# Sixteen-bit column addresses and 44 copied columns a step in a graph-network layer

## The chip, the cores and the metric

One core of one Trainium2 chip. The metric is the device time of one execution in microseconds (us). Three executions of the kernel before took 1896.46, 1897.21 and 1897.28 us; the median is 1897.21.

The engines: PE (TensorE) multiplies matrices, DVE (VectorE) and ACT (ScalarE) copy and do arithmetic by elements, POOL (GpSimd) issues the gathers, SP (SyncE) issues the other transfers. Each has its own queue of instructions and runs it in order. An engine's queue also runs instructions that touch no data path, such as loads of registers (TENSOR_LOAD); the profile shows these under DVEq, ACTq and so on, and doesn't count them as busy.

## What is computed

One layer of message passing on a graph of 12500 nodes with 64 features and 212500 edges with 32 features, sorted by destination, then a residual and a normalization:

```python
def _mlp(x, W1, b1, W2, b2):
    return jax.nn.relu(x @ W1 + b1) @ W2 + b2
msg_in = jnp.concatenate([nodes[row], nodes[col], edge_features], axis=-1)
messages = _mlp(msg_in, mW1, mb1, mW2, mb2)
aggregated = jax.ops.segment_sum(messages, col, num_segments=nodes.shape[0])
upd_in = jnp.concatenate([nodes, aggregated], axis=-1)
return _mlp(upd_in, uW1, ub1, uW2, ub2)
...
x = _layernorm(x + _L0_gnn_ref(...), axis=-1)
```

Here `row` is `src` and `col` is `dst`. All numbers are float32. The costly part is `nodes[row]`: for each edge the 64 features of its source, at an address that only the data tells.

## The kernel before

The edges are cut into 554 groups of 384 (G, GE), each of three tiles of 128 edges. The main loop (L560) makes one step for each group. Step k puts three pieces of work on PE, of three groups: `turn` of group k, `hidden` of group k-2, `sums` of group k-4.

- `gather` (L146): for each tile of a group, POOL issues one indirect DMA (L149) that fetches the 128 source rows from HBM into `own.s`, a ring of eight buffers. A gather of group g waits until PE has turned a group seven or eight before it. Groups are fetched four steps ahead (AHEAD), but POOL's own queue holds nothing besides, so it may run as far ahead as the ring allows.
- `onehot` (L329, VectorE) writes beside the rows, for each edge, which of 32 destinations of the group's window it has.
- `turn` (L341) transposes rows and one-hot columns on PE; ACT copies the result into `own.st` (L351), where a column is an edge: 64 source features, 32 one-hot rows, 32 edge features (these loaded by SP, L289).
- `hidden` (L366) multiplies these columns with the weights on PE; ACT applies the relu (L377).
- `sums` (L394, L399) adds up the messages of each window; VectorE adds them to `agg` and the counts to `own.xc` (L406, L407).
- `places` (L301, L308) and `windows` (L315, L320), once in four steps, prepare the destinations' part of the weights. The starts of four windows are loaded into registers by one TENSOR_LOAD (L301).
- `update` (L413 to L458), some 25 times, finishes 512 nodes: two matmuls, relu, second layer, statistics, normalization, store. Its steps stand in line with the main loop's.

For some groups the first of the three tiles isn't gathered. The list COPIED (L81) names them. The kernel holds all nodes' features transposed in SBUF (`own.xc`, one column of 4 bytes by 64 partitions a node), and `fetch` (L475) copies the sources of such a tile column by column straight into `own.st`: a copy of 64 x 4 bytes from a dynamic address, by VectorE (L503) or by ACT (L505). From step 18 (BEGIN) on each step copies 40 columns (COLS), in four batches: VectorE 8 and 12, ACT 12 and 8. Ahead of each batch one TENSOR_LOAD (issued at L490) reads the batch's addresses from `indices` into as many registers. So of every 3.2 steps one tile is copied and not gathered: 164 tiles, and 1497 gathers are left of 1661. For a copied group ACT's L351 is in two parts, since the copied columns must stay.

The addresses: `indexes` (L462) has SP load the node numbers of eight steps (SPAN) as 32-bit integers, `addresses` (L469, L473 on VectorE) turns them in place into byte addresses (times 4, plus `own.at`), two steps before they are used.

In a step's program order VectorE has L406, L407, in every fourth step L320 four times, then L329, the load and copies of its first batch, the load and copies of its second. ACT has L351, L377, then its two batches. Every engine may run ahead of or behind the others by about two steps, as far as buffers in PSUM and SBUF allow.

Of the kernel before, what the change touches and what calls it, by code (L numbers as in the profile page):

```python
# [11 lines left out]
BF16 = mybir.dt.bfloat16  # L12
I32 = mybir.dt.int32
U8 = mybir.dt.uint8
AF = mybir.ActivationFunctionType
ALU = mybir.AluOpType
ET = mybir.EngineType
# [3 lines left out]
P = 128  # L21
N = 12500
# [9 lines left out]
GE = TG * P  # L32
# [8 lines left out]
NP = N + 44  # L41
# [5 lines left out]
TIMES = 4  # L47
BEGIN = 18
CHECKED = 8
VCOLS = (8, 12)  # L50
ACOLS = (12, 8)
COLS = sum(VCOLS + ACOLS)
SPAN = 8


# [25 lines left out]
COPIED = []  # L81
while BEGIN - (-P * (len(COPIED) + 1) // COLS) < G - SHORT:
    COPIED.append(BEGIN - (-P * (len(COPIED) + 1) // COLS))


class Own:
# [4 lines left out]
    def __init__(self, nc, ctx):  # L91
        def on(name, *shape, of=nc.sbuf_tensor):
            return ctx.enter_context(of(name, list(shape), F32)).ap()

        self.s = [on(f"own_s{i}", P, TG, D + W) for i in range(RING)]
        self.st = [on(f"own_st{i}", P, SB * GE) for i in range(BLOCKS)]
        self.wm = [on(f"own_wm{i}", P, H) for i in range(NW)]
        self.h = [on(f"own_h{i}", P, TG, H) for i in range(NH)]
        self.ident = on("own_ident", P, P)
        self.one = on("own_one", P, 1)  # L100
        self.at = (nc.sbuf_base + 31) // 32 * 32
        self.xc = on("own_xc", P, NP)

        self.ps = [[on(f"own_ps{i}{k}", P, 512, of=nc.psum_tensor) for k in range(3)]
                   for i in range(2)]

# [2 lines left out]
def ordered(ctx: ExitStack, tc: tile.TileContext, a, own, ok):  # L109
# [3 lines left out]
    nc = tc.nc  # L113
# [3 lines left out]
    iop = ctx.enter_context(tc.tile_pool(name="iota_ps", bufs=1, space=PSUM))  # L117
    ups = ctx.enter_context(tc.tile_pool(name="upd_ps", bufs=1, space=PSUM))
    ixp = ctx.enter_context(tc.tile_pool(name="index", bufs=2))
    early = ctx.enter_context(ExitStack())  # L120
    temp = early.enter_context(tc.tile_pool(name="temp", bufs=1))
    ident, wm = own.ident, own.wm
    xc = own.xc[: D + 2]
    xc_bytes = own.xc.bitcast(U8)

# [9 lines left out]
    def after(first, *others):  # L135

        tc.declare_no_dep(first.ins, group="quiet", reason="waits for the last of a step")
        for i in others:
            tc.add_manual_dep(
                first.ins, i.ins.name,  # L140
                mybir.DependencyInfo(mybir.DependencyClass.Sync, mybir.DependencyReason.DATA),
                reason="the kernel's own rings",
            )
        return first
# [77 lines left out]
    for f, (g0, g1) in zip(firsts_f, halves):  # L222
# [20 lines left out]
    nc.scalar.activation(agg.rearrange("p (a b) -> p a b", a=P),  # L243
                         zero.unsqueeze(1).to_broadcast([P, P, NP // P]), AF.Copy)
    wc = const.tile([H, H], F32, name="wc")

    starts, xws, indices, columns_by = {}, {}, {}, {}

    up = None

# [41 lines left out]
    def columns(g):  # L292
        t, c = own.st[g // SB % BLOCKS], (g % SB) * GE
        return t, c, sum(tiles_of(g))
# [40 lines left out]
    def turn(g, ps):  # L335
# [9 lines left out]
        def copy(step):  # L345
# [4 lines left out]
            copies = [  # L350
                after(nc.scalar.activation(t[r, c : c + n][:, m], xt[r, m], AF.Copy), step)  # L351
                for r, m in (apart if g in columned else whole)
# [8 lines left out]
    def hidden(g, ps):  # L361
# [11 lines left out]
        def relu(step):  # L373
            hidden_by[g] = step
            h = own.h[g % NH]
            if len(set(sizes)) == 1:
                relu_by[g] = [nc.scalar.activation(h, pre, AF.Relu)]  # L377
            else:
                relu_by[g] = [nc.scalar.activation(h[:p, j, :], pre[:p, j, :], AF.Relu)
                              for j, p in enumerate(sizes)]  # L380
# [32 lines left out]
    def update(base, p, n):  # L413
# [8 lines left out]
        def first(xin):  # L422
# [3 lines left out]
            u = up.tile([H, CH], F32, name="u")  # L426
            nc.scalar.activation(u[:, :q], u_ps[:, :q], AF.Relu, bias=ub1)  # L427
            nc.vector.tensor_tensor(xin[:p, :n], xin[:p, :n],
# [3 lines left out]
        def second(xu):  # L432
# [12 lines left out]
            rstd = up.tile([P, 4], F32, name="rstd")  # L445
            nc.scalar.activation(rstd[:p, :n], mv[:p, :n, 1], AF.Sqrt, bias=eps[:p])  # L446
            return y, mv, rstd
# [13 lines left out]

    def indexes(i):  # L462

        n = min(SPAN * COLS, P * len(COPIED) - i * SPAN * COLS)
        if n > 0:
            indices[i] = ixp.tile([1, SPAN * COLS], I32, name="index")
            nc.sync.dma_start(indices[i][:, :n], a["src_copied"][:, i * SPAN * COLS :][:, :n])

    def addresses(i):  # L469

        if i in indices:
            t = indices[i][:, : min(SPAN * COLS, P * len(COPIED) - i * SPAN * COLS)]
            nc.vector.tensor_scalar(t, t, 4.0, float(own.at), ALU.mult, ALU.add)  # L473

    def fetch(k):  # L475

        i, n = divmod(k - BEGIN, SPAN)
        if i < 0:
            return
        if n == 0:  # L480
            indexes(i + 1)
        if n == SPAN - 2:
            addresses(i + 1)
        c0 = (k - BEGIN) * COLS
        for engine, count in [*((ET.DVE, c) for c in VCOLS), *((ET.Activation, c) for c in ACOLS)]:
            count = min(count, P * len(COPIED) - c0)
            if count <= 0:
                return
            b = c0 - i * SPAN * COLS
            _, v = nc.values_load_multi_w_load_instructions(  # L490
                indices[i][0:1, b : b + count], engines=[engine],
                min_val=own.at, max_val=own.at + 4 * (N - 1),
                skip_runtime_bounds_check_because="a source is one of the nodes",
            )
            for q, at in zip(range(c0, c0 + count), v):
                g, c = COPIED[q // P], q % P
                t, first_c, _ = columns(g)
                o = t.bitcast(U8)[:D, 4 * (first_c + c) : 4 * (first_c + c + 1)]
                x_at = xc_bytes[:D, bass.ds(at - own.at, 4)]
                by = columns_by.setdefault(g, {})  # L500
                new = engine not in by
                if engine == ET.DVE:
                    by[engine] = nc.vector.tensor_copy(o, x_at)  # L503
                else:
                    by[engine] = nc.scalar.activation(o, x_at, AF.Copy)  # L505
                after(by[engine], *([hidden_by[g - BLOCKS * SB]] if new else []))
            c0 += count

    waiting = [(closes, update(base, p, n)) for base, p, n, closes in PLAN]
    now = []  # L510
# [44 lines left out]
    places(0)  # L555
    windows(0, ups.tile([H, CH], F32, name="u_ps")[:, :H], False)[1]()
    indexes(0)
    made = summed = 0

    for k in range(G):  # L560
        if k < BITS:
            bit(k)
        if k == CHECKED:
            addresses(0)
            combined()
            ordered_edges()
            early.close()
            up = ctx.enter_context(tc.tile_pool(name="upd", bufs=2))
# [8 lines left out]
        else:  # L577
# [6 lines left out]
            for _ in range(2):  # L584
                if made <= k:
                    step((hidden, made))
                    made += 1
        onehot(k + 2)
        fetch(k)
        if k + AHEAD < G:  # L590
            gather(k + AHEAD)
# [285 lines left out]
@with_exitstack  # L877
def gnn_layer(ctx: ExitStack, nc, a):
    own = Own(nc, ctx)
    tc = ctx.enter_context(tile.TileContext(nc))  # L880
    flag = ctx.enter_context(tc.tile_pool(name="flag", bufs=1))
    ok = flag.tile([1, 1], I32, name="ok")
    with tc.manual_schedule():
        ordered(tc, a, own, ok)
    good = nc.values_load(ok[0:1, 0:1], min_val=0, max_val=1,
                          skip_runtime_bounds_check_because="a comparison's result")
    with tc.If(good == 0):
        with tc.manual_schedule():
            unordered(tc, a, own)
# [35 lines left out]
```

## Time and profile before

| | |
|---|---|
| median of three executions | 1897.21 us |
| profiled execution: its time | 1895.48 us |
| its span, first to last instruction | 1893.5 us |
| granted TensorE clock, mean | 0.969 |
| PE, busy | 1361.4 us (72%) |
| VectorE, busy | 1492.9 us (79%) |
| ACT, busy | 1550.7 us (82%) |
| POOL, busy | 1417.6 us (75%) |
| gathers (L149) | 1497, 946 ns each |
| column copies by VectorE (L503) | 10500, 897.7 us busy |
| column copies by ACT (L505) | 10492, 1057.1 us busy |
| ACT's copy of a turned group (L351): 96x384; 96x256 and 32x128 | 480 ns; 379 and 268 ns |
| address computation (L473) | 66, 0.37 us each |

How to read the views. A group's line has: code line, engine, operation, tile written <- tiles read, count | busy us, mean ns of one instruction | idle time of the engine just before, and what ended most of it. "issue" means that the engine waited for nothing that the profile shows: its queue was busy with something else, for example with a load of registers. A timeline line has start, duration, engine, line, operation, count, and in brackets the idle time before. Copies overlap on an engine: one lasts 190 ns from start to end, but the next starts some 80 ns after it (twelve take about 1.0 us), so busy time divided by count is below the mean. A line of a table by stretches has for each engine busy us and count, then clock, DMA share and GB/s. A line of a source's instructions has count, then shortest, median and longest in ns, then first and last start.

### The profile page before, as it was taken

The numbers are of one execution on the slowest core, as the hardware profiler recorded it, in microseconds if no ns is written. First come the engines' busy times: TensorE is split into PE (matmuls) and PEld (weight loads), VectorE is DVE, ScalarE is ACT, GpSimd is POOL, SyncE is SP. The second block draws the span as 40 slices with busy tenths as digits, with TensorE's granted clock in tenths as the row PEclk, the third lists the DMA queues.
The fourth block names the chain that finished last, engine by engine and source line by source line (L and its number), as shares of the span: only waits on it lengthen the run. The fifth ranks groups of instructions, "written<-read, shape, count | busy, mean of one in ns | idle before, by whom it ended". The sixth has DMA issues, their size and how long they took to land. (4 is left out here: it accounts for less than half of the span.)

```text
span 1893.5 us, 58044 instructions
## 1 busy us (share of the span) xinstructions
PE 1361.4 (72%) x12209; PEld 1193.4 (63%) x12209; DVE 1492.9 (79%) x13761; ACT 1550.7 (82%) x11818; POOL 1417.6 (75%) x1504
## 2 busy tenths in 40 slices
PE   3776777677777777677676776877767767767777
PEld 3666666666666666666665666666666656666665
DVE  3578888778888788887888878878888887888873
ACT  3489889888888888988988888889888888898882
POOL 7777777777777777777777777777777777777774
PEclk9999999999999999999999999999999999999999
DMA  6322222222222222222222222222222222222221
GB/s 136 73 46 45 46 48 44 50 43 48 46 45 48 47 43 50 45 46 44 48 50 43 48 46 45 46 48 44 50 44 47 47 48 44 47 44 50 44 47 29
DMA packets 68440, 92.50 MB, mean 49 GB/s; under 512 B 30893, under 2 KB 38350, under 8 KB 68078
## 3 DMA queue, kind: packets, MB, share of 16 engines
q0 software_dynamic: 47904, 49.12, 14.7%
q1 hardware_dynamic: 19260, 39.12, 7.4%
q14 instruction: 260, 2.13, 0.4%
q8 instruction: 102, 1.67, 0.4%
q10 hardware_dynamic: 914, 0.46, 0.1%
HBM read 85.29 MB, written 3.20 MB: 47 GB/s over the span
## 5 line engine op out<-in xcount | busy, mean ns | idle before, releaser
L149 POOL DMA_INDIRECT own_s<-in_x,src_sb x1497 | 1416.8, 946 | 457.3 <-issue 407.5
L503 DVE COPY own_st<-own_xc 64x4 uint8 x10500 | 897.7, 190 | 231.0 <-issue 217.9
L505 ACT ACTIVATE own_st<-own_xc 64x4 uint8 x10492 | 1057.1, 194 | 18.2 <-issue 15.2
L341 PE MATMUL own_ps<-own_ident,own_s 128*96 128x128 f32 x1661 | 289.5, 285 | 496.0 <-DMA own_s<-in_x,src_sb 157.9
L341 PEld LDWEIGHTS own_ps<-own_ident,own_s 128*96 128x96 f32 x1661 | 169.3, 132 | 566.1 <-ACT own_h L377 240.7
L394 PE MATMUL own_ps<-own_s,own_h 128*128 128x128 f32 x3322 | 480.5, 283 | 4.1 <-ACT own_h L377 2.9
L366 PE MATMUL own_ps<-own_wm,own_st 128*128 128x128 f32 x3322 | 479.4, 283 | 0.0
L351 ACT ACTIVATE own_st<-own_ps 96x384 f32<-96x384 f32 (+2 forms) x718 | 293.2, 408 | 205.8 <-PE own_ps L399 104.7
L394 PEld LDWEIGHTS own_ps<-own_s,own_h 128*128 128x128 f32 x3322 | 432.6, 199 | 6.3 <-ACT own_h L377 4.7
L366 PEld LDWEIGHTS own_ps<-own_wm,own_st 128*128 128x128 f32 x3322 | 432.1, 199 | 1.4 <-issue 0.5
L377 ACT ACTIVATE own_h<-own_ps 128x384 f32<-128x384 f32 x553 | 263.9, 477 | 16.0 <-PE own_ps L366 16.0
L399 PE MATMUL own_ps<-own_s,own_one 128*1 128x32 f32 x3322 | 190.1, 194 | 0.0
L320 DVE COPY own_wm<-own_ps 32x128 f32<-32x128 f32 x550 | 156.9, 285 | 5.6
L399 PEld LDWEIGHTS own_ps<-own_s,own_one 128*1 128x1 f32 x3322 | 114.5, 84 | 69.4 <-issue 6.2
L329 DVE TENSOR_TENSOR own_s<-iota,dlc 128x96 f32<-128x96 f32 x554 | 142.4, 258 | 14.3 <-issue 0.2
L406 DVE TENSOR_TENSOR agg<-own_ps,agg 128x32 f32 x554 | 105.1, 190 | 59.5 <-PE own_ps L399 25.9
L407 DVE TENSOR_TENSOR own_xc<-own_ps,own_xc 1x32 f32 x554 | 101.2, 183 | 30.6 <-PE u_ps L425 11.4
L308 DVE COPY xw<-own_xc 66x32 f32 x554 | 73.0, 207 | 15.5 <-DMA own_xc<-in_xT 9.8
L315 PE MATMUL own_ps<-w1b,xw 66*128 66x128 f32 (+1 forms) x276 | 69.1, 333 | 0.0
L446 ACT ACTIVATE rstd<-mv,eps 128x4 f32<-128x4 f32 (+1 forms) x25 | 7.4, 297 | 55.3 <-DVE mv L444 55.3
L437 PE MATMUL u_ps<-u,u 128*128 128x64 f32 (+1 forms) x196 | 50.1, 399 | 0.5 <-ACT u L427 0.5
L437 PEld LDWEIGHTS u_ps<-u,u 128*128 128x128 f32 (+1 forms) x196 | 47.1, 324 | 2.2 <-ACT u L427 0.9
(62 smaller groups left out, 276.7 us busy)
## 6 DMA issues: line engine op xcount, KB each, us to landing
own_st<-in_efT SPq DMA_DIRECT2D x138, 192.0 KB
own_s<-in_x,src_sb POOLq DMA_INDIRECT x1497
xin<-in_x SPq DMA_DIRECT2D x24, 128.0 KB
out<-o SPq DMA_DIRECT2D x24, 128.0 KB
own_xc<-in_xT SPq DMA_DIRECT2D x12, 179.2 KB
index<-in_src_copied SPq DMA_DIRECT2D x65, 1.2 KB
dlc_i<-in_dst_cols SPq DMA_DIRECT2D x1, 831.0 KB
own_xc<-in_xT SPq DMA_DIRECT2D x4, 179.5 KB
```

The source lines that it names most:

```text
L149: nc.gpsimd.indirect_dma_start(out=s[:p, j, :D], out_offset=None, in_=x[:, :], in_offset=bass.IndirectOffsetOnAxis(ap=src_sb[:p, g * TG + ...
L320: c = nc.vector.tensor_copy(wm[g % NW][D : D + W, :], wp[i * W : (i + 1) * W, :])
L329: places_by[g] = nc.vector.tensor_tensor(own.s[g % RING][:, :, D:], iota.unsqueeze(1).to_broadcast([P, TG, W]), dlc[:, g * TG : (g + 1) * ...
L341: nc.tensor.transpose(xt[:, j * P : j * P + p], s[:p, j, :], ident[:p, :p])
L351: after(nc.scalar.activation(t[r, c : c + n][:, m], xt[r, m], AF.Copy), step)
L366: nc.tensor.matmul(pre[:p, j, :], t[:, c + j * P : c + j * P + p], wm[g % NW], start=True, stop=True)
L377: relu_by[g] = [nc.scalar.activation(h, pre, AF.Relu)]
L394: did.append(nc.tensor.matmul(sg, h[:p, j, :], s[:p, j, D:].unsqueeze(1).to_broadcast([p, TIMES, W]), start=j == 0, stop=j == len(sizes) - 1))
L399: did.append(nc.tensor.matmul(counted, own.one[:p], s[:p, j, D:], start=j == 0, stop=j == len(sizes) - 1))
L406: after(nc.vector.tensor_tensor(agg[:, at], sg[:, 0, :], agg[:, at], ALU.add), step),
L503: by[engine] = nc.vector.tensor_copy(o, x_at)
L505: by[engine] = nc.scalar.activation(o, x_at, AF.Copy)
```

## The change

The addresses become 16-bit integers. `addresses` writes them into a tile of its own (`address`, two buffers), converting on the way; so that the largest address is below 65536, `own.xc` becomes the first tensor in SBUF, and the space at the start of SBUF that is kept for descriptors of POOL's transfers is set to 8 KB a partition, less than by default. A step copies 44 columns: VectorE 16 and 8, ACT 16 and 4, each batch with one load. In the array of node numbers each batch is filled up to a multiple of eight, so that each batch starts at a multiple of 16 bytes (48 slots a step for 44 columns).

```diff
+U16 = mybir.dt.uint16
...
-VCOLS = (8, 12)
-ACOLS = (12, 8)
+VCOLS = (16, 8)
+ACOLS = (16, 4)
 COLS = sum(VCOLS + ACOLS)
+LOADS = 8
+SLOTS = sum(-c // LOADS * -LOADS for c in VCOLS + ACOLS)
...
+        self.at = (nc.sbuf_base + 31) // 32 * 32
+        self.xc = on("own_xc", P, NP)
+        assert self.at + 4 * N <= 1 << 16
         self.s = [on(f"own_s{i}", P, TG, D + W) for i in range(RING)]
...
-        self.at = (nc.sbuf_base + 31) // 32 * 32
-        self.xc = on("own_xc", P, NP)
...
+    adp = ctx.enter_context(tc.tile_pool(name="address", bufs=2))
...
-        n = min(SPAN * COLS, P * len(COPIED) - i * SPAN * COLS)
-        if n > 0:
-            indices[i] = ixp.tile([1, SPAN * COLS], I32, name="index")
-            nc.sync.dma_start(indices[i][:, :n], a["src_copied"][:, i * SPAN * COLS :][:, :n])
+        if i * SPAN * COLS < P * len(COPIED):
+            indices[i] = ixp.tile([1, SPAN * SLOTS], I32, name="index")
+            nc.sync.dma_start(indices[i], a["src_copied"][:, i * SPAN * SLOTS :][:, : SPAN * SLOTS])
...
-            t = indices[i][:, : min(SPAN * COLS, P * len(COPIED) - i * SPAN * COLS)]
-            nc.vector.tensor_scalar(t, t, 4.0, float(own.at), ALU.mult, ALU.add)
+            addresses_by[i] = adp.tile([1, SPAN * SLOTS], U16, name="address")
+            nc.vector.tensor_scalar(addresses_by[i], indices.pop(i), 4.0, float(own.at),
+                                    ALU.mult, ALU.add)
...
-        c0 = (k - BEGIN) * COLS
-        for engine, count in [*((ET.DVE, c) for c in VCOLS), *((ET.Activation, c) for c in ACOLS)]:
-            count = min(count, P * len(COPIED) - c0)
+        c0, b = (k - BEGIN) * COLS, n * SLOTS
+        for engine, most in [*((ET.DVE, c) for c in VCOLS), *((ET.Activation, c) for c in ACOLS)]:
+            count = min(most, P * len(COPIED) - c0)
             if count <= 0:
                 return
-            b = c0 - i * SPAN * COLS
             _, v = nc.values_load_multi_w_load_instructions(
-                indices[i][0:1, b : b + count], engines=[engine],
+                addresses_by[i][0:1, b : b + count], engines=[engine],
...
             c0 += count
+            b += -most // LOADS * -LOADS
...
+    def slots(s):
+        n = -len(s) // (SPAN * COLS) * -SPAN
+        s = padded(s, n * COLS, 0).reshape(n, COLS)
+        parts, c = [], 0
+        for m in VCOLS + ACOLS:
+            parts.append(np.pad(s[:, c : c + m], ((0, 0), (0, -m % LOADS))))
+            c += m
+        return np.concatenate(parts, 1).reshape(1, n * SLOTS)
...
-    nc = bacc.Bacc("TRN2", target_bir_lowering=False, num_devices=1)
+    nc = bacc.Bacc("TRN2", target_bir_lowering=False, num_devices=1,
+                   dynamic_dma_scratch_size=1 << 13)
```

More of the change, by code (lines that the diff above doesn't have):

```diff
@@ L245, in ordered @@
     wc = const.tile([H, H], F32, name="wc")
-    starts, xws, indices, columns_by = {}, {}, {}, {}
+    starts, xws, indices, addresses_by, columns_by = {}, {}, {}, {}, {}
     up = None
@@ L905 @@
         "src": padded(v["src"], NT * P, 0).reshape(NT, P).T,
-        "src_copied": np.concatenate([v["src"][g * GE :][:P] for g in COPIED])[None],
+        "src_copied": slots(np.concatenate([v["src"][g * GE :][:P] for g in COPIED])),
         "dst_cols": padded(v["dst"], G * TG * P, -1).reshape(G * TG, P).T,
```

## The prediction

> **What bounds the kernel now.** I read the page's sums first, then the costliest groups, POOL's waits and timeline, VectorE's waits, and last the loads of registers, which the sums leave out.
>
> ```profile
> PE 1361.4 (72%) x12209; PEld 1193.4 (63%) x12209; DVE 1492.9 (79%) x13761; ACT 1550.7 (82%) x11818; POOL 1417.6 (75%) x1504
> ...
> L149 POOL DMA_INDIRECT own_s<-in_x,src_sb x1497 | 1416.8, 946 | 457.3 <-issue 407.5
> L503 DVE COPY own_st<-own_xc 64x4 uint8 x10500 | 897.7, 190 | 231.0 <-issue 217.9
> ```
>
> ACT looks busiest, but the share of busy time misleads. POOL's 1416.8 busy and 457.3 idle us make 1874 of the span's 1893.5, and the idle part is "issue": it waits for nobody. Its timeline, first in the opening (before any column is copied by VectorE), then in the middle:
>
> ```profile
> 21.30 0.95 POOL L149 DMA_INDIRECT own_s<-in_x,src_sb  x1 [0.30 <-issue]
> 22.55 0.94 POOL L149 DMA_INDIRECT own_s<-in_x,src_sb  x1 [0.30 <-issue]
> ...
> 1002.36 0.94 POOL L149 DMA_INDIRECT own_s<-in_x,src_sb  x1 [0.30 <-issue]
> 1003.60 0.94 POOL L149 DMA_INDIRECT own_s<-in_x,src_sb  x1 [0.30 <-issue]
> 1004.85 0.94 POOL L149 DMA_INDIRECT own_s<-in_x,src_sb  x1 [0.30 <-issue]
> ```
>
> A gather starts every 1.249 us, from the first to the last (1497 x 1.249 = 1870). In POOL's list of waits the longest wait for PE is 0.3 us, the gap that is there anyway, so the ring of eight buffers never holds a gather back. POOL sets the pace; the rest follows, and after the last gather's end (1875.7) some 18 us are left. The chain of waits starts from the last instruction and shows only this tail's engines; it doesn't name POOL.
>
> Second is VectorE, between 80 us (its first column) and 1846 (its last):
>
> ```profile
> 80.00:1846.00 1766.00, 1284.21 (x11584) 1127.82 (x11581) 1442.75 (x13528) 1513.39 (x11756) 1335.36 (x1414) 0.97 0.22 46
> ...
> DVE own_st L503 <- issue: 217.9, 585, 0.9
> ...
> 997.95 0.66 DVE L503 COPY own_st<-own_xc 64x4 uint8 x8 [0.23 <-issue]
> 999.12 1.00 DVE L503 COPY own_st<-own_xc 64x4 uint8 x12 [0.50 <-issue]
> ```
>
> It is busy 1442.75 of 1766, and 231 more go to gaps ahead of the copies, where its queue is reading registers: 95% used, against ACT's 86% (1513) with 15 us of such gaps. So the change must be followed on VectorE, though POOL sets the end.
>
> **Gathers.** The list COPIED grows from 164 tiles (525 steps x 40 / 128) to 180 (525 x 44 / 128), each one gather less: 1497 to 1481. 16 x 1.249 = 20.0 us less on POOL. No queue order changes there.
>
> **Copies.** 180 x 128 = 23040 columns at 44 a step are 523 steps and 28 columns more: VectorE 12576 (+2076), ACT 10464 (-28). On VectorE the 12-run above takes 1.00 us with a 0.15 tail, so a further copy in a run is about 78 ns: 2076 x 0.078 = +162 us. The address computation L473 goes from 320 to 384 elements, 0.37 to about 0.45 us, 66 times: +6. ACT gains 16 split copies of L351 (268 + 379 against 480 ns): +3, less 28 columns. The index load on SP has the same count with 1.5 KB for 1.2, issued eight steps ahead. One wait changes: L473 used to write in place, and now writes a buffer of its own that the loads of the span before the last must have left. Behind it in VectorE's queue stand the step's copies, and PE waits for those; but those loads ended six steps earlier, and ACT runs no more than two or three steps behind VectorE, so I cost it at nothing.
>
> **Loads of registers.** The durations, by line and engine, in narrow windows where the batch is known (4 starts; 8 columns; 12 columns), and a single register at the end:
>
> ```profile
> L301 DVEq TENSOR_LOAD <-start_i x139: 340/344/594, 13.8 to 1863.6; - x139
> ...
> L490 DVEq TENSOR_LOAD <-index x1: 597/597/597, 1002.9 to 1002.9; - x1
> ...
> L490 DVEq TENSOR_LOAD <-index x1: 847/847/847, 1004.2 to 1004.2; - x1
> ...
> L885 DVEq TENSOR_LOAD <-ok x1: 313/313/313, 1887.0 to 1887.0; - x1
> ```
>
> 1, 4, 8, 12 registers: 313, 344, 597, 847 ns. Three registers more cost 31 ns within the first four; each further four cost 250. So the price goes by reads of four 32-bit numbers, 16 bytes, and hardly by registers. The trace cannot say whether a read is 16 bytes or four registers, since all its numbers are 32 bits wide. Bound below: by bytes, 16 sixteen-bit numbers are 597 and 8 are 344 (at 10 ns a register more, some 680 and 385). Bound above: by fours of registers, 847 + 250 = 1097 and 597. I take the lower: one register costs nearly as much as four, as one read of a whole row would, and a rule by registers has to explain why the first four are nearly free.
>
> [...]
>
> What is seen of a load is what its cover leaves. The second load starts some 4 copies before the first batch ends: cover about 0.44 us, and 0.09 from its end to the first copy; 847 + 90 - 440 = 0.50, the gap at 999.12. After: 385 + 90 - 440 = 0.04, so most of the 180 us of these gaps go (the other 46 stand before the first batch). The first load is covered by L406, L407 and L329, 0.85 us when VectorE is behind: 680 + 90 fits. If that cover is gone (VectorE waiting for PE), 0.2 to 0.3 are seen, but then VectorE isn't late. ACT: 12 and 8 at 783 and 545 become 16 and 4, about 630 and 310, under L351 and L377 as now.
>
> **VectorE's new sum.** Busy 1443 + 162 + 6 = 1611, gaps about 35: 1646. From 676.4 to 716.5, where the kernel catches up after an update, VectorE was busy 33.9 and in gaps 5.1 of 40.1 us, 97%: that is how full it can be. 1646 / 0.97 = 1697, against the 1746 that POOL now leaves (1766 - 20). It fits with 49 us to spare; gaps could reach 83 us (0.16 a step) before it binds. ACT with 1516 and PE with 1284 fit.
>
> **Layout.** Own.xc goes first in SBUF so that addresses fit 16 bits, and POOL's scratch for descriptors is cut to 8 KB. I cost both at nothing: two or three gathers are in flight at 1.25 us each. If gathers had to wait for an earlier landing (some 1.6 us after POOL's end, by the first transposes of a group), the pace would go towards 2.5 us.
>
> **Sum.** 1893.5 - 20.0 = 1873.5 span; 1895.48 was that execution's time, 2.0 more, and the median shown is 1.7 above it: 1877.2, or -1.05%. What can be told from no change is 0.2%, 4 us.
>
> **Rivals.**
> 1. Slower: loads priced by fours of registers. Second load 597 + 90 - 440 = 0.25 x 524 = 130 us of gaps. First load 1097 + 90 - 850 = 0.33, on three steps in four (the fourth has L320's 1.18 us as cover): 130. VectorE: 1611 + 260 = 1871, over the 1746, and it decides from 83 us of gaps. Span 80 + 1871 to 1929 (at 97%) + 47.5, about 2000 to 2056; 2025 as time. For: four by four is as good a reading of 313, 344, 597, 847. Against: the nearly free first four.
> 2. The lower price holds, but VectorE's margin of 49 us is eaten: copies at 85 ns (897.7 / 10500) add 15, gaps of 80 instead of 35 add 45, and updates, whose steps run in line on VectorE, do the rest. It paces at (1626 + 80) / 0.97 = 1759, 13 over POOL: 1886 span, 1890; up to 1905. For: 95% used today. Against: today's 97% was reached while PE fed it.
> 3. VectorE's copies hold POOL. If each added copy stopped gathers for its 78 ns: +162 - 20, about 2039. Against: gathers take 0.95 us at 21.30 without columns and 0.94 at 1002 between them. [...]
> 4. The smaller scratch stalls gathers, or something not listed: over 1950.
>
> **How the numbers follow.** Forecast 0.70; rival 2 0.12 (of it 0.06 faster, 0.03 same, 0.03 slower); rival 1 0.13; rival 3 0.02; rival 4 0.03. Faster 0.76, same 0.03, slower 0.21. The range 1868 to 1908 holds the forecast (1872 to 1882 alone) and rival 2, 0.82; the rest lies far above and is left out.
>
> **What would show it.** Right: 1481 gathers, still 1.25 us apart; VectorE's loads near 600 to 700 and 345 to 400; gaps at L503 under 80 us; VectorE busy near 1660 of the span (88%). Wrong: loads near 1100 and 600 with gaps over 250 (rival 1); gathers that wait for PE for microseconds (VectorE or PE paces); gathers longer than 0.95 us (rivals 3, 4).

## The result, and the profile after

The changed kernel takes 3937.86 us (median of 4, 3934.33 to 3943.24) against 1896.84 for the kernel before: 2.076 times as long, 95% interval 2.073 to 2.080. The forecast was 1877. From the page of the changed kernel, the span, the busy sums, and the groups of the gathers and of VectorE's column copies:

```profile
span 3932.6 us, 60013 instructions
...
PE 2142.4 (54%) x12209; PEld 1873.6 (48%) x12209; DVE 1663.5 (42%) x15837; ACT 1597.2 (41%) x11806; POOL 1399.0 (36%) x1488
...
L153 POOL DMA_INDIRECT own_s<-in_x,src_sb x1481 | 1398.2, 944 | 2491.8 <-PE own_ps L403 2078.4
L506 DVE COPY own_st<-own_xc 64x4 uint8 x12576 | 1033.2, 172 | 2124.7 <-issue 1928.3
```

No engine is even 55% busy. The gathers are 16 fewer, as planned, and each lasts what it lasted; but POOL now waits 2078 us for PE. And ahead of VectorE's copies stand 2125 us of gaps in place of 231, again put down to "issue". VectorE's timeline of the changed kernel, two steps with four batches and what lies between:

```profile
2005.59 1.23 DVE L506 COPY own_st<-own_xc 64x4 uint8 x16 [2.70 <-issue]
2007.98 0.69 DVE L506 COPY own_st<-own_xc 64x4 uint8 x8 [1.16 <-issue]
2008.59 0.17 DVE L410 TENSOR_TENSOR agg<-own_ps,agg 128x32 f32 x1
2008.79 0.18 DVE L411 TENSOR_TENSOR own_xc<-own_ps,own_xc 1x32 f32 x1
2008.90 1.18 DVE L324 COPY own_wm<-own_ps 32x128 f32<-32x128 f32 x4
2010.09 0.26 DVE L333 TENSOR_TENSOR own_s<-iota,dlc 128x96 f32<-128x96 f32 x1
2012.48 1.23 DVE L506 COPY own_st<-own_xc 64x4 uint8 x16 [2.13 <-issue]
2015.36 0.66 DVE L506 COPY own_st<-own_xc 64x4 uint8 x8 [1.65 <-issue]
```

What runs in these gaps are the loads of registers (count, then shortest, median, longest in ns), in windows that hold one of each: VectorE's load of 16, its load of 8, and ACT's of 4:

```profile
L493 DVEq TENSOR_LOAD <-address x1: 3589/3589/3589, 2008.8 to 2008.8; - x1
...
L493 DVEq TENSOR_LOAD <-address x1: 1833/1833/1833, 2013.1 to 2013.1; - x1
...
L493 ACTq TENSOR_LOAD <-address x1: 880/880/880, 2008.5 to 2008.5; - x1
```

Sixteen registers take 3589 ns and eight 1833: (3589 - 1833) / 8 = 220 ns a register. Before, 32-bit loads of 8 and 12 took 597 and 847. The profile puts 192 us of the 2125 down to ACT, but counted in the trace, 1041 of VectorE's 1048 loads end less than 0.1 us before the first copy of their batch starts: the copies wait for the loads. Do the gaps account for the time? The table by stretches, from VectorE's first column to its last:

```profile
79.00:3876.00 3797.00, 2058.25 (x11568) 1801.40 (x11563) 1612.19 (x15595) 1559.24 (x11743) 1330.32 (x1411) 0.63 0.10 22
```

VectorE is busy 1612 us there, and with 2125 of gaps its queue is full for 3737 of 3797 us, 98%. Before, it was 1443 + 231 in 1766. So the gaps grew by 1894 and the busy time by 169, together 2063, against 2039 that the span grew. PE stands behind VectorE: its turn of a group (L345) starts 0.10 us after VectorE has written the group's one-hot columns (L333), in 481 of the 514 steps that are left without the first and last 20.

```profile
2017.07 0.26 DVE L333 TENSOR_TENSOR own_s<-iota,dlc 128x96 f32<-128x96 f32 x1
...
2017.43 0.85 PE L345 MATMUL own_ps<-own_ident,own_s 128*96 128x128 f32 x3 [3.16 <-issue]
```

And POOL stands behind PE: bursts of five gathers at the old spacing (the first three and the next burst's first are shown), then a long wait for PE to free a pair of buffers.

```profile
2007.09 0.94 POOL L153 DMA_INDIRECT own_s<-in_x,src_sb  x1 [11.51 <-PE own_ps L403]
2008.33 0.94 POOL L153 DMA_INDIRECT own_s<-in_x,src_sb  x1 [0.31 <-issue]
2009.58 0.94 POOL L153 DMA_INDIRECT own_s<-in_x,src_sb  x1 [0.30 <-issue]
...
2021.52 0.94 POOL L153 DMA_INDIRECT own_s<-in_x,src_sb  x1 [8.49 <-PE own_ps L403]
```

### The profile page after: what moved, and what is told of

It reads as the page before. It is cut to its first block, busy times and chain, and to the rows that moved or that the text cites. A ratio compares the mean times of both kernels' runs of the same rounds, so it can differ in the third digit from the quotient of the medians.

```text
span 3932.6 us, 60013 instructions
## 1 busy us (share of the span) xinstructions
PE 2142.4 (54%) x12209; PEld 1873.6 (48%) x12209; DVE 1663.5 (42%) x15837; ACT 1597.2 (41%) x11806; POOL 1399.0 (36%) x1488
## 5 line engine op out<-in xcount | busy, mean ns | idle before, releaser
L506 DVE COPY own_st<-own_xc 64x4 uint8 x12576 | 1033.2, 172 | 2124.7 <-issue 1928.3
L345 PE MATMUL own_ps<-own_ident,own_s 128*96 128x128 f32 x1661 | 427.5, 389 | 1695.0 <-issue 1246.8
L345 PEld LDWEIGHTS own_ps<-own_ident,own_s 128*96 128x96 f32 x1661 | 229.8, 172 | 1804.3 <-issue 1343.5
L398 PE MATMUL own_ps<-own_s,own_h 128*128 128x128 f32 x3322 | 764.6, 397 | 4.2 <-ACT own_h L381 3.6
L370 PE MATMUL own_ps<-own_wm,own_st 128*128 128x128 f32 x3322 | 764.0, 397 | 0.0
L398 PEld LDWEIGHTS own_ps<-own_s,own_h 128*128 128x128 f32 x3322 | 721.2, 312 | 6.2 <-ACT own_h L381 5.2
L370 PEld LDWEIGHTS own_ps<-own_wm,own_st 128*128 128x128 f32 x3322 | 712.4, 309 | 5.5 <-issue 0.5
L403 PE MATMUL own_ps<-own_s,own_one 128*1 128x32 f32 x3322 | 237.9, 221 | 0.0
L403 PEld LDWEIGHTS own_ps<-own_s,own_one 128*1 128x1 f32 x3322 | 146.8, 94 | 109.7 <-issue 93.6
L333 DVE TENSOR_TENSOR own_s<-iota,dlc 128x96 f32<-128x96 f32 x554 | 142.4, 258 | 14.2
L428 PE MATMUL u_ps<-agg,wc 128*128 128x512 f32 (+1 forms) x50 | 44.7, 992 | 59.2 <-DVE agg L410 59.2
```

The source lines that it names most:

```text
L333: places_by[g] = nc.vector.tensor_tensor(own.s[g % RING][:, :, D:], iota.unsqueeze(1).to_broadcast([P, TG, W]), dlc[:, g * TG : (g + 1) * ...
L345: nc.tensor.transpose(xt[:, j * P : j * P + p], s[:p, j, :], ident[:p, :p])
L370: nc.tensor.matmul(pre[:p, j, :], t[:, c + j * P : c + j * P + p], wm[g % NW], start=True, stop=True)
L398: did.append(nc.tensor.matmul(sg, h[:p, j, :], s[:p, j, D:].unsqueeze(1).to_broadcast([p, TIMES, W]), start=j == 0, stop=j == len(sizes) - 1))
L403: did.append(nc.tensor.matmul(counted, own.one[:p], s[:p, j, D:], start=j == 0, stop=j == len(sizes) - 1))
```

## The experiments

The theory: VectorE's queue is the pace, because its 16-bit loads go one register at a time, at the 220 ns found above. Rivals: the batch of sixteen or the new tile is what costs; the layout; ACT's loads, which grew as well; the four added columns.

The experiments ran on five chips where the kernel before itself takes 2550 to 2670 us; in its runs there, engines also pause in the middle of batches (last section). Times are therefore given as ratios to the kernel before on the same chip. The loads take what they took on the chip of the result, which is called the first chip here (most of them within 1%; VectorE's of the changed kernel: shortest 1820 and median 2711 ns there, 1820 and 2707 on the first chip).

**32-bit addresses again, all else as changed** (twice)

```diff
-            addresses_by[i] = adp.tile([1, SPAN * SLOTS], U16, name="address")
+            addresses_by[i] = adp.tile([1, SPAN * SLOTS], I32, name="address")
```

> The changed kernel with one edit: the address tile is 32-bit again; batches (16 and 8, 16 and 4), slots, layout and 44 columns stay. Theory 'width': a load reads 32-bit numbers four at a time and 16-bit numbers one at a time (about 222 ns each). Then VectorE's loads are near 1097 and 597 ns, ACT's near 1030 and 300, VectorE's gaps about 0.5 us a step (260 us), and the time is 2000 to 2060 us, the price of the prediction's first rival. Theory 'batch' (a load of sixteen, or the padded slots, or the tile of its own is what costs): VectorE's loads stay over 1800 ns and the time over 3500. If the 44 columns cost nothing by themselves: 1877.

> The run with 32-bit addresses and 44 columns again, timed in rounds beside the kernel before. 'Theory of adjacent words': loads 1090 and 595 ns; by the prediction's model for these loads VectorE needs 1612 us busy and about 260 of gaps, 1.05 to 1.09 times the time of the kernel before. Rival (44 columns are free once loads are fast): 0.99.

2786.76 us in a single execution, with the kernel before at 2551.45; then, on another of the chips, 2799.35 (median of 4) against 2560.42, 1.093 times (1.088 to 1.099). The loads of the first of these runs, ACT's 4 and 16 (shortest and longest of the two) and VectorE's 8 and 16:

```profile
L493 ACTq TENSOR_LOAD <-address x2: 311/666/1021, 1301.0 to 1302.6; - x2
L493 DVEq TENSOR_LOAD <-address x2: 597/846/1094, 1301.6 to 1303.0; - x2
```

The same batches of 16 and 8, in the same tile and slots, are back at four for 250 ns: 1094 and 597, the upper bound of the prediction (1097 and 597) within 3 ns. That clears the batch, the slots and the tile. The absolute times were missed, since the expectation didn't foresee that the kernel before is slower there; the ratio lies at or just above the 1.05 to 1.09 expected. So on these chips 44 columns in these batches lose even with fast loads. No run shows what they would take on the first chip.

**The changed kernel on such a chip**

> The changed kernel itself on a chip of the experiments. If slow loads on VectorE alone set its step (7.1 us) there as well: 3900 to 4010 us, loads 3590 and 1820 ns, and of the distance to the run with 32-bit addresses (2787 and 2799 on such chips) some 1150 to 1200 us belong to the reading one by one. Rival (other delays of these chips add to it in proportion, as to the kernel before): 1.35 times 3938, over 5000.

3975.38 us, 1.559 times the kernel before (1.553 to 1.566). VectorE's group in this run:

```profile
L506 DVE COPY own_st<-own_xc 64x4 uint8 x12576 | 1032.9, 172 | 2125.1 <-issue 1954.6
```

The gaps are 2125 again, and the time is within 1% of the first chip's. The pauses of these chips are hardly there in this run: inside VectorE's batches, after the first copy, the trace has 5 us of gaps, as on the first chip, against 228 us in the 32-bit version. Of the 1.559, the 32-bit version keeps 1.093; 3975 - 2793 (the mean of its two times) = about 1180 us is what the reading one by one adds there. As the 32-bit version has the pauses and this run doesn't, that isn't its price on the first chip.

**40 columns in the old batches, 16-bit**

```diff
-VCOLS = (16, 8)
-ACOLS = (16, 4)
+VCOLS = (8, 12)
+ACOLS = (12, 8)
```

> The changed kernel with the old batches: 40 columns, VectorE 8 and 12, ACT 12 and 8, addresses 16-bit. Theory 'width': VectorE's loads 1820 and 2710 ns, ACT's about 2540 and 1710. Gaps by the cover model: first 1820 + 90 - 850 = 1.06 on three steps in four, second 2710 + 90 - 440 = 2.36, so 3.16 a step; with 2.75 busy 5.9 a step: 526 x 5.9 + 127 = 3230 us. Theory 'batch' (sixteen in one load is what costs): loads of 8 and 12 near 600 and 850, time near 1900.

3477.72 us, 1.36 times the kernel before. VectorE's loads are about 1825 and 2706 ns, ACT's 1713 and 2538: 16-bit loads of the old sizes are as slow for each register ((2706 - 1825) / 4 = 220 ns on VectorE). The gaps are 1790 us where the covers gave 3.16 x 525 = 1660; the time is 8% over the expectation.

**The layout alone**

```diff
+        self.at = (nc.sbuf_base + 31) // 32 * 32
+        self.xc = on("own_xc", P, NP)
         self.s = [on(f"own_s{i}", P, TG, D + W) for i in range(RING)]
...
-        self.at = (nc.sbuf_base + 31) // 32 * 32
-        self.xc = on("own_xc", P, NP)
...
-    nc = bacc.Bacc("TRN2", target_bir_lowering=False, num_devices=1)
+    nc = bacc.Bacc("TRN2", target_bir_lowering=False, num_devices=1,
+                   dynamic_dma_scratch_size=1 << 13)
```

> The kernel before with the layout alone: own.xc first in SBUF, 8 KB for descriptors; addresses 32-bit in place, 40 columns. Theory 'width': layout costs nothing, 1897 us within 4, gathers 1.249 us apart. Theory 'layout' (the smaller descriptor space or the place of own.xc slows gathers or copies): a time well above, over 1950, with longer gathers or copies.

2557.02 against 2551.45, 1.0006 times (0.998 to 1.004). The place of own.xc and the smaller space for descriptors cost nothing.

**ACT's loads fast, VectorE's slow**

```diff
...
+            for e, t in ((ET.DVE, U16), (ET.Activation, I32)):
+                addresses_by[i][e] = adp.tile([1, SPAN * SLOTS], t, name=f"address{e.name}")
...
-                addresses_by[i][0:1, b : b + count], engines=[engine],
+                addresses_by[i][engine][0:1, b : b + count], engines=[engine],
...
```

> The changed kernel, with ACT reading its addresses from a second, 32-bit tile (one more address computation of 0.45 us in eight steps on VectorE); VectorE reads 16-bit ones. Theory 'VectorE alone': VectorE's queue is full (1612 us busy and 2125 of gaps in the 3797 between its first and last column), so the time stays between 3800 and 3950 although ACT's loads fall from 3370 and 880 to about 1030 and 300 ns. Rival 'both': the two engines' loads take turns in setting the step through PE, and the time falls by more than 150 us, below 3780.

3997.78 us, next to 3975.38 for the changed kernel on such a chip (measured later, on another). ACT's loads of this run (all: shortest, median, longest) and its column copies:

```profile
L496 ACTq TENSOR_LOAD <-addressActivation x1047: 305/318/1212, 113.2 to 3923.8; - x175
...
L511 ACT ACTIVATE own_st<-own_xc 64x4 uint8 x10464 | 1054.5, 190 | 107.9 <-issue 97.9
```

ACT's gaps ahead of its columns fall from 1312 us (the changed kernel on such a chip) to 108, and the time doesn't fall. VectorE alone sets it; ACT's slow loads were hidden behind it. The time is 1.2% over the expected 3950.

**What makes a load slow.** The 32-bit version, with the addresses eight bytes apart, and then contiguous but shifted by one word:

```diff
-            addresses_by[i] = adp.tile([1, SPAN * SLOTS], I32, name="address")
+            t = adp.tile([1, SPAN * SLOTS, 2], I32, name="address")
+            addresses_by[i] = t[:, :, 0]
```

```diff
-            addresses_by[i] = adp.tile([1, SPAN * SLOTS], I32, name="address")
+            t = adp.tile([1, SPAN * SLOTS + 4], I32, name="address")
+            addresses_by[i] = t[:, 1 : 1 + SPAN * SLOTS]
```

> The run with 32-bit addresses and 44 columns once more, with one edit: the 32-bit addresses lie eight bytes apart, so that a batch isn't contiguous. Theory 'width' (32-bit numbers are read four at a time, wherever they lie): loads of 16 and 8 stay near 1090 and 595 ns on VectorE. Rival 'adjacent' (four are read at a time when they fill one row of 16 bytes without gaps; anything else goes one by one): 3590 and 1820 ns, as in the changed kernel. Rival 'bytes' (each row of 16 bytes read costs about 250 ns): twice the rows, near 2100 and 1090 ns.

> The run with 32-bit addresses and 44 columns, contiguous, but shifted by one word, so that each batch starts 4 bytes past a multiple of 16. If four adjacent words from wherever the batch starts are read at once: 1090 and 595 ns as aligned. If aligned rows are read: one more row each, 1340 and 845. If an unaligned batch goes one by one: 3590 and 1820.

3982.97 and 3993.38 us, as slow as the changed kernel. VectorE's loads of 8 and 16, in the run with the words apart:

```profile
L494 DVEq TENSOR_LOAD <-address x1: 1832/1832/1832, 1302.5 to 1302.5; - x1
...
L494 DVEq TENSOR_LOAD <-address x1: 3592/3592/3592, 1305.1 to 1305.1; - x1
```

and in the run that is one word off:

```profile
L494 DVEq TENSOR_LOAD <-address x1: 3601/3601/3601, 1301.1 to 1301.1; - x1
...
L494 DVEq TENSOR_LOAD <-address x1: 1844/1844/1844, 1305.6 to 1305.6; - x1
```

So "width" falls: 32-bit numbers cost as much as if read one by one, too, when they aren't adjacent, or when the batch doesn't start at a multiple of 16 bytes. In these runs only adjacent 32-bit words that fill aligned rows of 16 bytes took 250 ns for four more registers (1094 and 597 ns for 16 and 8); 16-bit words, words apart and words off a row took some 220 ns for each (3589 to 3601 and 1832 to 1844 ns).

**42 columns, first without and then with aligned batches.** VectorE 12 and 8, ACT 12 and 10; the second run on the 32-bit version with batches filled up to four words:

```diff
-VCOLS = (8, 12)
-ACOLS = (12, 8)
+VCOLS = (12, 8)
+ACOLS = (12, 10)
```

```diff
-LOADS = 8
+LOADS = 4
```

> The kernel before with 42 columns in batches that keep 32-bit addresses: VectorE 12 and 8, ACT 12 and 10. 8 gathers less, 10 us of POOL. VectorE's sum is lower than before (the order takes some 60 us of gaps), ACT's rises by 1050 copies of 0.0955 us, 100 us. If POOL paces: 0.995 of the kernel before. If ACT binds (1513 + 100 of 1756 us): 1.00 to 1.02.

> 42 columns again (VectorE 12 and 8, ACT 12 and 10), 32-bit, with each batch filled up to a multiple of four words, so that all start at a multiple of 16 bytes. Theory 'aligned rows': VectorE's loads 845 and 595 ns in every step, ACT's 783 and 783; what the unaligned run of 42 lost (1.13 of the kernel before) comes back, 0.98 to 1.02. Rival (the two more columns on ACT are what cost): it stays over 1.08.

The first missed its expectation: 2899.01 us, 1.130 times (1.123 to 1.137). Its step has 42 words, 168 bytes, so every other step starts 8 bytes past a row. VectorE's loads there: 8 of an aligned step; 12 of an aligned step and 8 of the step before it; 12 of a step that isn't aligned:

```profile
L490 DVEq TENSOR_LOAD <-index x1: 597/597/597, 1306.6 to 1306.6; - x1
...
L490 DVEq TENSOR_LOAD <-index x2: 852/1352/1851, 1301.8 to 1305.0; - x2
...
L490 DVEq TENSOR_LOAD <-index x1: 2732/2732/2732, 1308.8 to 1308.8; - x1
```

Fast (597, 852) and slow (1851, 2732) loads alternate within one kernel. Filled up to whole rows, the same 42 columns take 2668.83 against 2664.41, 1.000 times (0.997 to 1.004): all that was lost came back. One part of the expectation failed: ACT's load of 10 was to take 783 ns like its load of 12, and takes more. Both, shortest and longest of two:

```profile
L493 ACTq TENSOR_LOAD <-address x2: 785/886/988, 1303.8 to 1305.0; - x2
```

Its first eight registers are two whole rows, 545 ns as in the kernel before; the two left over add 443, some 220 each, the price of the slow loads. So a batch should also be a multiple of four.

**The order of VectorE's batches**, 12 and 8 for 8 and 12, in the kernel before:

> The kernel before with VectorE's batches in the other order, 12 and 8 for 8 and 12; nothing else. By the cover model the second load falls to 597 + 90 - 440 = 0.25 us of gap for 0.5, the first rises to 847 + 90 - 850 = 0.09 where VectorE is behind: gaps ahead of L503 go from 231 us to about 165, and the time stays at that of the kernel before, since POOL paces it. Rival: the gaps stay at 231, since a load shows in full whatever it follows.

2675.86 us against 2669.34, one execution each. Gaps ahead of L503 are 305 us, where the run of the layout alone, in the old order, has 363: 58 less, near the 66 expected, though on another chip. But more than half of both are pauses of these chips, inside batches: ahead of the batches' first copies stand 131 and 166 us, 35 less. The gaps move the way that the covers say, and no more is shown.

**How many columns, with fast loads.** 44 with ACT at 12 and 12; 36 (VectorE 8 and 8, ACT 12 and 8); 32 (8 and 8, 8 and 8); 24 (8 and 4, 8 and 4), all aligned and 32-bit, the constants alone edited:

> 44 columns, 32-bit, aligned, the four added ones on ACT: VectorE 12 and 8, ACT 12 and 12. VectorE has the sum of the kernel before or less; ACT has 2096 copies more, 200 us. If VectorE's load and copies were what made 44 columns cost 1.09 of the kernel before: 0.98 to 1.03. If ACT is as full: 1.04 to 1.10.

> 36 columns, 32-bit, aligned: VectorE 8 and 8, ACT 12 and 8. 17 tiles more are gathered (21 us of POOL), VectorE copies four columns a step less and reads one row less. If POOL paces here as in the profile before: 1.01. If VectorE, ACT and PE pace on this chip: 0.92 to 0.98, so that the copied columns are already past their best number there.

> 32 columns, 32-bit, aligned: VectorE 8 and 8, ACT 8 and 8, four ACT copies a step less than the run of 36. 1530 gathers, 1911 us of POOL. If ACT's and VectorE's queues pace on these chips: 0.88 to 0.92 of the kernel before (36 columns: 0.94). If 36 is where something else takes over: 0.93 to 0.96.

> 24 columns, 32-bit, aligned: VectorE 8 and 4, ACT 8 and 4. 1563 gathers, 1952 us of POOL, which then is near the end. If the column copies pace: 0.78 to 0.86 of the kernel before, not below 0.77 (POOL). If not: as the run of 32.

| columns | us | of the kernel before |
|---|---|---|
| 44, VectorE 24 | 2799.35 | 1.093 (1.088 to 1.099) |
| 44, ACT 24 | 2713.67 | 1.017 (1.009 to 1.024) |
| 42 | 2668.83 | 1.000 (0.997 to 1.004) |
| 36 | 2503.89 | 0.941 (0.935 to 0.948) |
| 32 | 2441.18 | 0.956 (0.952 to 0.960) |
| 24 | 2454.39 | 0.963 (0.958 to 0.967) |

The four added columns cost much less on ACT than on VectorE (1.017 against 1.093), though the two ratios come from different chips. And on these chips fewer copied columns than 40 are faster: the versions of 36, 32 and 24 beat the kernel before there. From 36 down the gain stops, against 0.78 to 0.92 expected for 32 and 24 if column copies were the pace (36 ran on one chip, 32 and 24 on another). From the pages, the gathers of the run of 36 and of the run of 24:

```profile
L153 POOL DMA_INDIRECT own_s<-in_x,src_sb x1514 | 1435.1, 948 | 1018.6 <-PE own_ps L403 383.9
```

```profile
L153 POOL DMA_INDIRECT own_s<-in_x,src_sb x1563 | 1479.7, 947 | 925.0 <-issue 403.9
```

POOL still idles 1019 and 925 us, far over its usual 0.31 us a gather (some 470), so it isn't the pace there either. What is stays open. On the chip of the first profiles, where POOL paces, 36 columns would by its 1514 gathers cost 17 x 1.249 = 21 us; that wasn't tried.

## Why the prediction was wrong

- **What bounds the kernel before**: held. Gathers stand 1.249 us apart whenever they are let go, before and after, and VectorE was the engine to follow.
- **Gathers and copies**: held. 1481 gathers; VectorE's busy time between its first and last column is 1612 us, where the sum gave 1611. That it is this close is luck: the copies' own time grew by 135 us and not 162, the address computation by 1 and not 6, and the difference is made up by instructions of different lines overlapping 30 us less than before.
- **Loads of registers**: this step failed. It read 344, 597 and 847 ns rightly as reads of four 32-bit numbers, and the 313 ns of a single register as one more such read; then it took 16-bit ones to be read by rows of 16 bytes (680 and 385), "bound above" by fours of registers (1097 and 597). They measured 3589 and 1833. Both bounds rested on the same belief, that a read always brings at least four. The row for a read that brings one stood in the same fence: 313 ns for one register, so 16 x 313 = 5.0 us as the outer bound, and the truth, 220 a register, lies between. The upper bound was right for what it described, aligned 32-bit loads of 16 and 8 (1094 and 597). And the profile before could have told. Its 554 groups make 138 loads of four starts and a last one of two, which the prediction's fence for L301 counts without showing its time:

```profile
L301 DVEq TENSOR_LOAD <-start_i x1: 540/540/540, 1863.6 to 1863.6; - x1
```

  Two registers take longer than four (344), and 540 - 313 = 227 ns for the second is near the 220 that the changed kernel pays for each. By the prediction's reading, two would lie between 313 and 344.
- **Cover**: held as a sum, in part by luck. With the measured loads the prediction's own covers give 3590 + 90 - 850 = 2.83 us on three steps in four, 1.18 less on the fourth, and 1830 + 90 - 440 = 1.48 for the second: 4.0 a step, 2100 us in 524 steps; the profile has 2125. By batches the trace has 1509 us ahead of the sixteen, where the covers give 1328, and 610 ahead of the eight, where they give 776. The first load's cover was smaller than 0.85 us (median gap 3.08), the second's larger than 0.44 (median gap 1.16), and the two errors cancel.
- **Rival 1**: right that VectorE's loads take over the pace, wrong in their price, which goes by single registers and not by fours. The gaps passed the 83 us from which it decides; it put them at 260 us, and they are 2125. It had a chance of 0.13, and the range left it out.
- **Layout, rivals 2 to 4**: layout at nothing held (1.0006), which clears the scratch of rival 4; its "something not listed: over 1950" is where the time fell. Gathers take 944 ns, 946 before, so nothing of rival 3 shows; it is a weak test, as copies and gathers both lie further apart in time than it supposed. Rival 2 never came into play.

## What to carry to other kernels

Where a trace shows the price of an instruction rising in steps (here 250 ns for every four registers), it shows the fast way of doing it, for the operands that it was given. It doesn't show that other operands stay on the fast way. The outer bound for operands that the trace doesn't have is the price of the slow way, here that of a single register times their number (313 x 16 = 5.0 us, where 3.59 was measured). Batches of numbers for registers belong in adjacent 32-bit words, a multiple of four of them, that start at a multiple of 16 bytes (here 597 ns for eight, against 1820 to 1851 where the words were 16-bit, apart or off a row), and a change of a count (40 to 42 words a step) can break that without touching a load (here 1.130 times the kernel before, and 1.000 once mended). And in these profiles loads of registers are in no busy sum: they are seen as idle time with "issue" as its cause (1928 of the 2125 us ahead of VectorE's copies).

## What the runs showed of the hardware

- On VectorE a load of registers from SBUF took 250 ns for every four more registers where they were aligned, adjacent 32-bit words, and about 220 ns each where they were 16-bit, eight bytes apart, or 4 or 8 bytes off a row (8 registers: 597 against 1820 to 1851 ns). Registers left over from the last four of an aligned batch cost about 220 ns each too (ACT: 988 for 10, 785 for 12; VectorE, before: 540 for 2, 344 for 4). ACT's loads are a little quicker: 783 for 12 aligned (VectorE 847), and 2532 one by one (VectorE 2706).
- The granted TensorE clock was 0.969 with PE 72% busy before, and 0.643 with PE 54% busy after; the mean of the same matmuls (L394 before, L398 after) went from 283 to 397 ns. PE waited for VectorE in most steps (481 of 514, by the one-hot columns above); what lowers the clock, and whether it cost any time, wasn't tested.
- On the chips of the experiments VectorE and ACT pause inside batches, where they wait for nothing that the profile shows. In the run of the layout alone the gaps inside VectorE's and ACT's batches are 197 and 282 us, in the profile before 5 and under 1, and in the changed kernel on such a chip 5 and 1: there the pauses are not seen. ACT's columns in the run of the layout alone, and a batch of 20 in the profile before:

```profile
1305.22 1.60 ACT L505 ACTIVATE own_st<-own_xc 64x4 uint8 x15
1307.75 0.30 ACT L505 ACTIVATE own_st<-own_xc 64x4 uint8 x2 [0.94 <-issue]
1308.48 0.21 ACT L505 ACTIVATE own_st<-own_xc 64x4 uint8 x1 [0.42 <-issue]
1309.19 0.30 ACT L505 ACTIVATE own_st<-own_xc 64x4 uint8 x2 [0.51 <-issue]
```

```profile
1005.52 2.00 ACT L505 ACTIVATE own_st<-own_xc 64x4 uint8 x20
```

The batch resumes at 1307.75, 1308.48 and 1309.19, 0.7 us apart, with no load of ACT between; VectorE's batch beside it resumes at 1307.75 and 1309.18. The granted clock of that run is 0.802, and the kernel before had 0.80 to 0.82 beside it, where the first chip gave it 0.969. What causes the pauses, and whether they are all that slows the kernel before there, isn't known.
